# A decoder layer on one core: the first entry's order, the experts' banks and the last sums rearranged

## The chip, the core and the metric

The kernel runs on one core of a Trainium2 chip. A core has five engines with queues of their own, which meet only through semaphores: PE (TensorE: matmuls and transposes, results in PSUM), DVE (VectorE), ACT (ScalarE), POOL (GpSimd) and SP (SyncE, here only for issuing DMAs). "PEld" is PE's weight load, which overlaps its matmuls. [...] The metric is the time of one execution on the device in microseconds (us), as the median of the runs.

## The reference

A pre-norm decoder layer in float32 on 16 entries (b) of 128 tokens by 256 features:

```python
x = x + self_attention(layernorm(x))            # 16 heads of 64: q, k, v 256 -> 1024, output 1024 -> 256
x = x + cross_attention(layernorm(x), ctx, mask) # 16 heads of 16, one key mask for all entries
xf = layernorm(x).reshape(2048, 256)
logits = xf @ gate_w.T + gate_b                  # 8 experts; RMS norm, softmax at temperature 0.5
g = max(softmax(...)); norm_g = g / (g + 1e-6)   # the largest gate only
h = gelu(einsum('nd,edh->neh', xf, w1) + b1)     # all 8 experts, 512 hidden each
y = einsum('neh,ehd->ned', h, w2) + b2
x = x + (y * norm_g).sum(axis=1)                 # every expert's output counts, with one common gate
```

As every expert is used with the same factor, the experts are one two-layer network with 4096 hidden features.

## The kernel before

**Attention.** Work is cut into 16 slots, one per entry, in `slot(s)`. A slot's steps are not issued where they stand in the code. `at(name, f, ...)` puts each into one heap with a due time, slot number x SLOT (28.2 us) + `DUE[name]`, and `run_slots` then issues all steps of all slots in the order of their due times. Since PE, DVE, ACT and POOL run under `manual_schedule`, that order is the order of each engine's queue. A step that evacuates a PSUM tile (`due`) has a due time of its own.

The names that matter here: q0, q1, k0, k1, v0, v1 are the projections of queries, keys and values in halves of 512 columns (functions `queries`, `keys`, `values`; the profile's tiles mm_qk and mm_v); q0e, ke0, ve0 and so on are their evacuations (queries on DVE, keys and values on ACT). S0 and S1 are the scores of half the heads each (tile sc). For each half, max is the negated maximum on DVE (L331), ex the exponentials on ACT in two groups of four (L337), r the reciprocal of the sums on DVE (L348) and mul the normalization on POOL (L352). T1a1 to T1b2 transpose the probabilities on PE (tr_p, L367), with copies on DVE (prT); SVa and SVb multiply with the values, SO is the output projection (mm_o, weights wo). xn1, LN1 and LN1c normalize a later entry's tokens, transpose them on PE and copy them out on ACT. "early" stands for the statistics of entries 2 and 3, a chain of small DVE operations; st0 to st11 are the others' statistics.

Ahead of the slots, without due times, stand the first entry's steps in program order: normalization of entry 0, its transposes (tr_x), then keys half 0, queries half 0, normalization of entry 1, keys half 1, queries half 1, values, with entry 1's transposes between. Slot 0 then starts with both halves of the scores. The weights wq and wk are loaded in quarters of 256 columns, wq by SP's queue, wk by ACT's; rowv (biases by row, spread to all partitions) and small bias columns (bqk) by POOL's. For every engine's DMAs the queue's order is the program's.

**Experts.** Tokens go in four blocks m of 512, hidden features in 16 pairs of blocks p. Each 2x2 block product is made by seven products in place of eight (a Strassen scheme): `hidden_first` and `hidden_last` make the hidden sums in banks ha, hb, he, hf, with sums u on DVE between and factors t after the GELUs; `summed(ns, ...)` adds the products numbered ns of the second layer into eight half-banks, two in each of the four tiles y0 to y3, by `ORDER = (2, 3, 4, 8, 1, 7, 5, 6)`: products 2 and 3 share y0, 4 and 8 y1, 1 and 7 y2, 5 and 6 y3. Product 8 occurs only where the first blocks were made plainly (m = 0). The second layer's products of step p are issued in the step after it. When block m - 1 is complete, in step p = 0 of block m (a seam), `finished` makes the final sums yT straight from the half-banks, one copy on ACT and seven or eight sums on DVE; `rest`, in steps 1 and 2, transposes half of yT on PE into the bank of "he", scales with the gate, adds the residual into ot on DVE and stores it. In the experts only PE has an order written out (`manual_schedule(engines={PE})`); DVE and ACT are ordered by the framework's scheduler, which starts ready operations by priority, earlier program order first. The framework also makes every reader and writer of one bank wait for each other.

Of the kernel before, what the change touches and what calls it, by code (L numbers as in the profile page):

```python
# [65 lines left out]
    cross=13.9, st0=14.3, st1=14.8, st2=15.6, st3=16.2, st4=17.4, st5=17.9, st6=18.4, st7=18.9,  # L66
    st8=20.0, st9=20.5, st10=21.0, st11=21.5, late=31.7,
)
PRE_STEPS = ("q0", "k0", "v0", "q1", "v1", "k1")
LATE_STATS = tuple(f"st{n}" for n in range(B - 4))  # L70

# [2 lines left out]
def decoder_layer(  # L74
# [57 lines left out]
    make_identity(nc, ident)  # L132


    xs = const.tile([P, B, D], F32, tag="xs", name="xs")
    wq = keep.tile([P, KD, HD1], F32, tag="k0", name="wq")
    wk = keep.tile([P, KD, HD1], F32, tag="k1", name="wk")
# [10 lines left out]

    load_tokens(0, 1)
    nc.scalar.dma_start(out=colv, in_=cols)  # L150
    for n in range(4):
        for w, src, q in ((wq, wq1, nc.sync), (wk, wk1, nc.scalar)):
            f = slice(n * 256, (n + 1) * 256)
            q.dma_start(out=w[:, :, f], in_=src[:, :, f])
    load_tokens(1, 1)
    for n in range(2):
        f = slice(n * 512, (n + 1) * 512)
        nc.sync.dma_start(out=wv[:, :, f], in_=wv1[:, :, f])
    nc.gpsimd.dma_start(out=rowv, in_=rows.partition_broadcast(P))
    nc.gpsimd.dma_start(out=msk, in_=mask)  # L160

    bqk2 = const.tile([P, 2, C2], F32, tag="bqk2", name="bqk2")
    for n, c0 in enumerate((BQ2, BK2)):
        for m in range(C2):
            for f in range(2):
                nc.gpsimd.dma_start(
                    out=bqk2[64 * f : 64 * f + 64, n, m : m + 1],
                    in_=cols[:, c0 + 2 * m + f : c0 + 2 * m + f + 1].rearrange(
                        "(a s) o -> a s o", s=32
                    )[:, :DH2],  # L170
                )
    def context(g):
        c = work.tile([P, KD, GT], F32, tag="ctx", name=f"ctx{g}")
        nc.sync.dma_start(out=c, in_=ctxT[g])
        return c
# [58 lines left out]
    def at(name, f, *a):  # L234


        if now[0] is None:
            f(*a)
        else:
            heapq.heappush(events, (now[0] * SLOT + DUE[name], next(count), now[0], f, a))  # L240

    def due(name, f, *a):

        if now[0] is None:
            with urgent():
                f(*a)
        else:
            at(name, f, *a)

    count = itertools.count()  # L250

# [121 lines left out]
    def self_norm(b):  # L373
        entry["xn1", b] = normalize(b, *first[b])

    def self_norm_transposed(b):
        xnT1 = ap.tile([P, KD, 1, T], F32, tag="xnT1", name="xnT1")
        transpose_tokens([entry.pop(("xn1", b))], xnT1, "LN1c")
        entry["xnT1", b] = xnT1

    def project(b, w, n, tag):
# [14 lines left out]
                )  # L396
        return entry[tag, b], mm

    def queries(b, n):
        qT, mm = project(b, wq, n, "qT")  # L400
        due(
            f"q{n}e",
            nc.vector.tensor_tensor,
            qT[:, 4 * n : 4 * n + 4, :],
            mm,
            col(BQ1 + 4 * n, 4).unsqueeze(2).broadcast_to([P, 4, T]),
            ALU.add,
        )

    def keys(b, n):  # L410
        kT, mm = project(b, wk, n, "kT")

        def out():
            for i in range(4):
                c = 4 * n + i
                nc.scalar.activation(
                    kT[:, c, :], mm[:, i, :], AF.Identity,
                    bias=bk1[:, c : c + 1], scale=DH1 ** -0.5,
                )

        due(f"ke{n}", out)

    def values(b, n):
        mm = psum_mm("mm_v")
        if n == 0:
            entry["v", b] = ap.tile([P, HD1], F32, tag="v", name="v")
        f = slice(n * 512, (n + 1) * 512)
        for k in range(KD):
            nc.tensor.matmul(  # L429
                mm,  # L430
                entry["xnT1", b][:, k, 0, :],
                wv[:, k, f],
                start=(k == 0),
                stop=(k == KD - 1),
            )
        due(f"ve{n}", nc.scalar.copy, entry["v", b][:, f], mm)

    def self_scores(b, half):

# [323 lines left out]
    def slot(s):  # L763


        for half in range(2):
            at(f"S{half}", self_scores, s, half)
            at(f"SV{'ab'[half]}", self_values, s, half)
            for n in range(2):
                at(f"T1{'ab'[half]}{n + 1}", self_transposed, s, half, n)  # L770
                if s >= 2:
                    at(f"T2{'ab'[half]}{n + 1}", cross_transposed, s - 2, half, n)
        at("SO", self_output, s)
        at("cvr", cross_value_rows, s)
        at("ck", cross_keys, s)
        normalize_outputs(s, s - 2 if s >= 2 else None)
        if s >= 1:
            at("LNx", cross_norm, s - 1)
            at("CQ", cross_queries, s - 1)
            at("CS", cross_scores, s - 1)  # L780
            at("CS", cross_softmax, s - 1)
        if s >= 2:
            at("CV", cross_values, s - 2)
            at("CO", cross_output, s - 2)
        if s >= 3:
            at("LN3", expert_norm, s - 3)
        if s + 2 < B:
            at("xn1", self_norm, s + 2)
            at("ab1", add_bias, s + 2, BO1)
            at("LN1", self_norm_transposed, s + 2)  # L790
        if s + 1 < B:
            for n in range(2):
                at(f"q{n}", queries, s + 1, n)
                at(f"k{n}", keys, s + 1, n)
                at(f"v{n}", values, s + 1, n)
        else:
            for n, name in enumerate(PRE_STEPS):
                copy = nc.vector.tensor_copy if name[0] == "q" else nc.scalar.copy
                out = f"q{name[1]}e" if name[0] == "q" else f"{name[0]}e{name[1]}"
                at(name, pre_hidden, n, copy, out)  # L800
        if s == 0:
            mv2 = variances(2)
            for i in range(2):
                at(f"early{i}", statistics, mv2[:, i, :], 2 + i)
            at("early", lambda: first.update(inverse_deviations(mv2, [2, 3])))
            at("cross", for_cross)
            mv = variances(B - 4)
            for i, name in enumerate(LATE_STATS):
                at(name, statistics, mv[:, i, :], 4 + i)

            def rest():
                first.update(inverse_deviations(mv, list(range(4, B))))

            at("late", rest)
# [7 lines left out]

    first = deviations([0])
    self_norm(0)
    add_bias(0, BO1)
    self_norm_transposed(0)

    nc.vector.tensor_scalar_mul(bk1, colv[:, BK1 : BK1 + C1], DH1 ** -0.5)
    keys(0, 0)
    queries(0, 0)  # L830
    first.update(deviations([1]))
    self_norm(1)
    add_bias(1, BO1)
    keys(0, 1)
    queries(0, 1)
    values(0, 0)
    self_norm_transposed(1)
    values(0, 1)

    hidden_keys = const.tile([P, T], U8, tag="hidden_keys", name="hidden_keys")  # L840
    masked = const.tile([P, 1], F32, tag="masked", name="masked")
# [205 lines left out]
                start=cleared(i // 2, begun), stop=(p == NP - 1), skip_group_check=True,  # L1047
            )

    def finished(m, sums, plain):  # L1050
        ys = {n: sums[0][i // 2][:, i % 2] for i, n in enumerate(ORDER)}
        yT = yp.tile([P, KD, MT], F32, tag="yT", name="yT")
        u = hp.tile([P, 4, HT], F32, tag="u", name="yu")
# [1 line left out]
        def plus(out, k, y, other):  # L1055
            nc.vector.scalar_tensor_tensor(out, y, b2[:, k : k + 1], other, ALU.add, ALU.add)  # L1056

        nc.scalar.copy(u[:, 0], ys[1])
        nc.vector.tensor_add(u[:, 1], u[:, 0], ys[6])
        nc.vector.tensor_add(u[:, 2], u[:, 1], ys[7])  # L1060
        nc.vector.tensor_add(u[:, 3], u[:, 1], ys[5])
        plus(yT[:, 0, :HT], 0, ys[2], u[:, 0])
        plus(yT[:, 0, HT:], 0, ys[3], u[:, 3])
        if plain:
            plus(yT[:, 1, :HT], 1, ys[4], u[:, 2])
            nc.vector.tensor_add(u[:, 2], u[:, 2], ys[8])
            plus(yT[:, 1, HT:], 1, ys[5], u[:, 2])
        else:
            plus(yT[:, 1, HT:], 1, ys[5], u[:, 2])
            plus(yT[:, 1, :HT], 1, ys[4], u[:, 2])  # L1070

        def rest(i, bank):
            tr = ps_h.tile([P, 4, P], F32, tag=bank, name="tr_y")
            for j in range(2):
# [29 lines left out]
    def experts():  # L1104
# [1 line left out]


        nonlocal ys
        rest = None
        xr = token_factors(0)  # L1110
        combine(2)
        combine(3)
# [4 lines left out]
        for m in range(NT // MT):  # L1117
            for p in range(0 if m else PRE, NP):
# [11 lines left out]
                    lgT = gate_logits()  # L1130
                if m == 0 and p == PRE + 3:
                    gate_transposed(lgT)
                if before is None:
                    summed_plain(1, PRE - 1, ys)
                else:
                    summed((7, 5, 6, 4), *before, ys)
                    if before[0] == NP - 1:
                        rest = finished(m - 1, ys, m == 1)
                if m == 0 and p in (PRE, PRE + 1):
                    combine(p - PRE)  # L1140
                if m == 0 and p == PRE + 3:
                    gates()
                if p in (1, 2) and rest is not None:
                    rest(p - 1, "he")
                before = now
        summed((1, 5, 7, 6, 2, 3, 4), *before, ys)
        rest = finished(m, ys, False)
        for i, bank in enumerate(("hb", "hf")):
            rest(i, bank)

# [66 lines left out]
```

## Time and profile before

| | us |
|---|---|
| median of 3 runs | 876.49 (876.48 to 878.98) |
| the profiled execution's own time | 877.13 |
| its span, first to last instruction | 875.3 |
| PE busy | 856.2 |
| DVE busy | 627.5 |
| ACT busy | 425.5 |
| POOL busy | 166.8 |

In the profile's lines, L390 is line 390 of the kernel, `out<-in` names tiles, "128x512 f32" are partitions and elements, and what stands in brackets is the idle time of the engine just before and what ended it. A timeline line gives start, length of the merged group, engine, line, operation, tiles and count. The chain that ended last is followed back from the last instruction, each time to what released it; its lines give start, length and engine.

### The profile page before, as it was taken

The numbers are of one execution on the slowest core, as the hardware profiler recorded it, in microseconds if no ns is written. First come the engines' busy times: TensorE is split into PE (matmuls) and PEld (weight loads), VectorE is DVE, ScalarE is ACT, GpSimd is POOL, SyncE is SP. The second block draws the span as 40 slices with busy tenths as digits, with TensorE's granted clock in tenths as the row PEclk, the third lists the DMA queues.
The fourth block names the chain that finished last, engine by engine and source line by source line (L and its number), as shares of the span: only waits on it lengthen the run. The fifth ranks groups of instructions, "written<-read, shape, count | busy, mean of one in ns | idle before, by whom it ended". The sixth has DMA issues, their size and how long they took to land.

```text
span 875.3 us, 15944 instructions
## 1 busy us (share of the span) xinstructions
PE 856.2 (98%) x5940; PEld 713.6 (82%) x5940; DVE 627.5 (72%) x1513; ACT 425.5 (49%) x1623; POOL 166.8 (19%) x179
## 2 busy tenths in 40 slices
PE   6999999999999999999999999999999999999997
PEld 5788888888888888888865558878888888878886
DVE  3887787878878787878877497775567656575655
ACT  2356755577565765567554613333333333433332
POOL 4224423343333423343231100000000000000000
PEclk9999999999999999999999999999999999999999
DMA  8800000000000000000140100000000000000000
GB/s 220 253 1 14 1 14 2 2 13 2 13 2 2 13 2 1 14 2 1 51 177 15 49 0 1 1 25 1 0 1 1 25 0 1 1 13 13 0 1 25
DMA packets 19406, 21.29 MB, mean 24 GB/s; under 512 B 9649, under 2 KB 15809, under 8 KB 18689
## 3 DMA queue, kind: packets, MB, share of 16 engines
q1 hardware_dynamic: 17728, 18.89, 6.9%
q10 hardware_dynamic: 1232, 1.09, 0.5%
q8 instruction: 47, 0.77, 0.4%
q0 software_dynamic: 368, 0.30, 0.3%
q14 instruction: 31, 0.25, 0.1%
HBM read 18.16 MB, written 2.10 MB: 23 GB/s over the span
## 4 chain that ended last, share of the span: by engine, by line
PE 89%; DVE 7%; issue 1%; ACT 1%; DMA 1%; POOL 0%; DVEq 0%; ACTq 0%; POOLq 0%
PE y L1004 18%; PE mm_qk L390 13%; PE mm_v L429 6%; PE tr_p L367 6%; PE mm_o L489 6%; PE he L1004 5%; PE hf L1004 5%; PE ha L1004 5%; PE sc L445 4%; PE po L469 3%; PE mm_h L753 3%; PE hb L1004 2%; PE sc L579 2%; PE po L618 2%; PE mm_q L557 2%; PE y L894 2%
## 5 line engine op out<-in xcount | busy, mean ns | idle before, releaser
L352 POOL TENSOR_TENSOR cpr<-cpr,rinv 128x512 f32<-128x512 f32 x64 | 68.5, 1072 | 219.6 <-DVE rinv L348 219.3
L337 ACT ACTIVATE cpr<-sc,nmax 128x128 f32<-128x128 f32 x256 | 89.9, 411 | 11.6 <-DVE nmax L331 11.6
L337 ACT ACTIVATE pr<-sc,nmax 128x128 f32<-128x128 f32 x256 | 90.8, 420 | 1.8 <-DVE nmax L331 1.8
L352 POOL TENSOR_TENSOR pr<-pr,rinv 128x512 f32<-128x512 f32 x64 | 66.0, 1043 | 74.6 <-DVE rinv L348 74.3
L331 DVE TENSOR_REDUCE nmax<-sc 128x8 f32<-128x1024 f32 x64 | 76.4, 1216 | 4.7 <-PE sc L445 4.7
L1034 DVE TENSOR_TENSOR c<-u,hf 128x256 f32<-128x256 f32 x56 | 23.6, 421 | 72.0 <-PE hf L1004 71.9
L1033 ACT ACTIVATE h<-u,colv 128x256 f32<-128x256 f32 x56 | 28.4, 507 | 88.2 <-DVE u L1020 86.4
L390 PEld LDWEIGHTS mm_qk<-xnT,wk 128*128 128x128 f32 x512 | 62.5, 196 | 9.2 <-issue 6.4
L258 ACT COPY xnT<-tr_x 128x256 f32<-128x256 f32 x42 | 15.6, 372 | 109.5 <-PE tr_x L316 109.5
L1004 PE MATMUL hf<-xt,w 128*128 128x256 f32 x224 | 66.9, 380 | 0.4 <-DVE u L1019 0.4
L1004 PE MATMUL y<-t,w 128*128 128x256 f32 x224 | 66.7, 379 | 0.0
L1004 PE MATMUL ha<-xnT,w 128*128 128x256 f32 x224 | 66.6, 379 | 0.0
L337 ACT ACTIVATION_READ_ACCUMULATOR pr<-sc,nmax 128x1 f32 x256 | 66.3, 259 | 0.0
L390 PE MATMUL mm_qk<-xnT,wk 128*128 128x128 f32 x512 | 64.2, 280 | 1.7 <-DMA wk<-in_wk 1.7
L337 ACT ACTIVATION_READ_ACCUMULATOR cpr<-sc,nmax 128x1 f32 x256 | 64.4, 251 | 0.0
L390 PE MATMUL mm_qk<-xnT,wq 128*128 128x128 f32 x512 | 64.2, 279 | 0.0
L1017 ACT COPY u<-ha 128x256 f32<-128x256 f32 x56 | 20.9, 373 | 86.8 <-PE ha L1004 86.8
L390 PEld LDWEIGHTS mm_qk<-xnT,wq 128*128 128x128 f32 x512 | 60.1, 193 | 3.0 <-issue 2.9
L429 PE MATMUL mm_v<-wv,xnT 128*128 128x512 f32 x128 | 60.2, 592 | 0.0
L1004 PE MATMUL y<-h,w 128*128 128x256 f32 x224 | 58.7, 381 | 1.5 <-DVE yT L1056 1.1
L489 PE MATMUL mm_o<-wo,atT 128*128 128x256 f32 x256 | 57.9, 379 | 0.0
L258 DVE COPY prT<-tr_p 128x512 f32<-128x512 f32 x64 | 39.7, 682 | 18.6 <-PE tr_p L367 18.6
(167 smaller groups left out, 1864.9 us busy)
## 6 DMA issues: line engine op xcount, KB each, us to landing
w<-in_w SPq DMA_DIRECT2D x8, 1024.0 KB, 5.4
ctx<-in_ctxT SPq DMA_DIRECT2D x8, 256.0 KB, 2.7
out_x<-ot SPq DMA_DIRECT2D x8, 256.0 KB, 2.2
xs<-in_x SPq DMA_DIRECT2D x3, 512.0 KB, 5.3
wk<-in_wk ACTq DMA_DIRECT2D x4, 256.0 KB, 8.5
wq<-in_wq SPq DMA_DIRECT2D x4, 256.0 KB, 10.2
wv<-in_wv SPq DMA_DIRECT2D x2, 512.0 KB, 7.7
wo<-in_wo SPq DMA_DIRECT2D x1, 1024.0 KB, 8.3
```

Source lines behind the costliest of these rows:

```text
L258: f(*a)
L331: nc.vector.tensor_reduce(w["nmax"], sc, AX.X, ALU.max, negate=True)
L337: nc.scalar.activation(w["pr"][:, i, :], sc[:, i, :], AF.Exp, bias=w["nmax"][:, i : i + 1], scale=1.0, accum_out=sums[:, j : j + 1],)
L352: nc.gpsimd.tensor_tensor(four, four, w["rinv", n].unsqueeze(2).broadcast_to([P, 4, T]), ALU.mult)
L367: nc.tensor.transpose(tr[:, j, :], w["pr"][:, 4 * n + j, :], ident)
L390: nc.tensor.matmul(mm[:, i, :], w[:, k, c * P : (c + 1) * P], xnT1[:, k, 0, :], start=(k == 0), stop=(k == KD - 1),)
L429: nc.tensor.matmul(mm, entry["xnT1", b][:, k, 0, :], wv[:, k, f], start=(k == 0), stop=(k == KD - 1),)
L445: nc.tensor.matmul(sc[:, j, c * T : (c + 1) * T], qT[r, 4 * half + c, :], kT[r, 4 * half + c, :], start=True, stop=True,)
L469: nc.tensor.matmul(po[j * DH1 : (j + 1) * DH1, c, :], v[:, h * DH1 : (h + 1) * DH1], prT[:, 4 * j + c, :], start=True, stop=True,)
L489: nc.tensor.matmul(mm[:, :D], atT[:, c, :], wo[:, c, :], start=(c == 0), stop=(c == C1 - 1))
L1004: nc.tensor.matmul(out, left[p // q][n - 1][:, p % q], rights[n - 1], **flags)
L1033: nc.scalar.activation(h[:, 1, 1], u[:, 3], AF.Gelu, bias=col(B1 + 2 * p + 1))
```

## The change

1. Loads: wk and wq in halves of 512 columns, all by SP's queue, wk's half before wq's, entry 1's tokens after the first pair; rowv after the small bqk loads on POOL's queue.
2. A tile of zeros is set on DVE first, and PE multiplies it eleven times by itself into a bank nobody reads.
3. The first entry's steps go into the heap as well, under slot 0, with due times of their own (FIRST_DUE, negative for those before the slots). Scores of half 0 come right after keys and queries of that half and keys of the next; the softmax steps of slot 0 have new due times. The additions of the output bias to entries 0 and 1 (fab0, fab1) come after the normalizations on POOL.
4. At a seam, `emptied` copies y0, y2 and y3 out on ACT and y1 on DVE, with high priority; `summed_up_later` makes the sums from the copies, one step later. `rest` follows in steps 2 and 3, between `hidden_last` and the second layer's last products, into the bank of "hb".
5. After the last step, `summed_last` issues the products in the order 1, 6, 2, 7, 4, 5, 3 with the sums between them.

```diff
+FIRST_DUE = dict(
+    fk0=-11.4, fq0=-9.5, fk0e=-9.4, fq0e=-7.7, fk1=-7.2, norm1=-7.0, S0=-5.4, fk1e=-5.3, fq1=-4.4,
+    max0=-4.0, ex0a=-2.7, fLN=-2.65, fq1e=-2.6, fv0=-2.3, fLNc=-1.4, r0a=-1.32, ex0b=-1.3,
+    mul0a=-1.2, S1=-0.6, fv0e=0.1, r0b=0.15, mul0b=0.2, max1=0.4, fv1=0.41, ex1a=1.65, fv1e=3.0,
+    r1a=3.1, mul1a=3.2, ex1b=3.6, cvre=5.0, r1b=5.1, mul1b=5.2, fab0=5.5, fab1=6.5,
 )
...
+    zeros = work.tile([P, T], F32, tag="xnT2", name="zeros")
+    nc.vector.memset(zeros, 0.0)
+    mm = psum_mm("mm_0")
+    for n in range(11):
+        nc.tensor.matmul(mm[:, :T], zeros, zeros, start=True, stop=True)
...
-    for n in range(4):
-        for w, src, q in ((wq, wq1, nc.sync), (wk, wk1, nc.scalar)):
-            f = slice(n * 256, (n + 1) * 256)
-            q.dma_start(out=w[:, :, f], in_=src[:, :, f])
-    load_tokens(1, 1)
+    for n in range(2):
+        f = slice(n * 512, (n + 1) * 512)
+        for w, src in ((wk, wk1), (wq, wq1)):
+            nc.sync.dma_start(out=w[:, :, f], in_=src[:, :, f])
+        if n == 0:
+            load_tokens(1, 1)
...
-    nc.gpsimd.dma_start(out=rowv, in_=rows.partition_broadcast(P))
     nc.gpsimd.dma_start(out=msk, in_=mask)
...
+    nc.gpsimd.dma_start(out=rowv, in_=rows.partition_broadcast(P))
...
+    def when(name):
+        s = now[0]
+        return s * SLOT + (FIRST_DUE[name] if s == 0 and name in FIRST_DUE else DUE[name])
...
         if s == 0:
+            for n in range(2):
+                at(f"fk{n}", keys, 0, n, "fk{}e")
+                at(f"fq{n}", queries, 0, n, "fq{}e")
+                at(f"fv{n}", values, 0, n, "fv{}e")
+                at(f"fab{n}", add_bias, n, BO1)
+            def second():
+                first.update(deviations([1]))
+                self_norm(1)
+            at("norm1", second)
+            at("fLN", self_norm_transposed, 1, "fLNc")
...
     self_norm(0)
-    add_bias(0, BO1)
     self_norm_transposed(0)
...
-    keys(0, 0)
-    queries(0, 0)
-    first.update(deviations([1]))
-    self_norm(1)
-    add_bias(1, BO1)
-    keys(0, 1)
-    queries(0, 1)
-    values(0, 0)
-    self_norm_transposed(1)
-    values(0, 1)
...
+    def emptied(sums, plain):
+        y0, y1, y2, y3 = sums[0]
+        yT = yp.tile([P, KD, MT], F32, tag="yT", name="yT")
+        u = rp.tile([P, 4, HT], F32, tag="xt", name="yu")
+        y4_8 = yT[:, 1].rearrange("p (n t) -> p n t", n=2)
+        with tc.high_priority():
+            nc.scalar.activation(
+                yT[:, 0].rearrange("p (n t) -> p n t", n=2), y0, AF.Identity, bias=b2[:, 0:1]
+            )
+            nc.scalar.copy(u[:, 0:2], y2)
+            nc.scalar.copy(u[:, 2:4], y3)
+            n = 2 if plain else 1
+            nc.vector.tensor_scalar_add(y4_8[:, :n], y1[:, :n], b2[:, 1:2])
+        return yT, u, plain
+
+    def summed_up_later(yT, u, plain):
+        y1, y7, y5, y6 = (u[:, n] for n in range(4))
+        def plus(y, other):
+            nc.vector.tensor_add(y, y, other)
+        plus(y6, y1)
+        plus(y7, y6)
+        plus(yT[:, 0, :HT], y1)
+        plus(yT[:, 1, :HT], y7)
...
+        plus(y5, y6)
+        plus(yT[:, 0, HT:], y5)
+        return yT
+
+    def summed_last(p, hr, sums):
...
+        completed(1)
         nc.scalar.copy(u[:, 0], ys[1])
+        completed(6)
         nc.vector.tensor_add(u[:, 1], u[:, 0], ys[6])
+        completed(2, 7)
         nc.vector.tensor_add(u[:, 2], u[:, 1], ys[7])
+        plus(yT[:, 0, :HT], 0, ys[2], u[:, 0])
+        completed(4)
+        plus(yT[:, 1, :HT], 1, ys[4], u[:, 2])
+        completed(5)
         nc.vector.tensor_add(u[:, 3], u[:, 1], ys[5])
+        plus(yT[:, 1, HT:], 1, ys[5], u[:, 2])
+        completed(3)
         plus(yT[:, 0, HT:], 0, ys[3], u[:, 3])
...
+                if p == 1 and out is not None:
+                    rest = finished(m - 1, summed_up_later(*out))
+                if p in (2, 3) and rest is not None:
+                    rest(p - 2, "hb")
...
                     if before[0] == NP - 1:
-                        rest = finished(m - 1, ys, m == 1)
+                        out = emptied(ys, m == 1)
...
-                if p in (1, 2) and rest is not None:
-                    rest(p - 1, "he")
...
-        summed((1, 5, 7, 6, 2, 3, 4), *before, ys)
-        rest = finished(m, ys, False)
+        rest = finished(m, summed_last(*before, ys))
```

More of the change, by code (lines that the diff above doesn't have):

```diff
@@ L239, in at @@
         else:
-            heapq.heappush(events, (now[0] * SLOT + DUE[name], next(count), now[0], f, a))
+            heapq.heappush(events, (when(name), next(count), now[0], f, a))
     def due(name, f, *a):
@@ L374, in self_norm, with self_norm_transposed @@
         entry["xn1", b] = normalize(b, *first[b])
-    def self_norm_transposed(b):
+    def self_norm_transposed(b, name="LN1c"):
         xnT1 = ap.tile([P, KD, 1, T], F32, tag="xnT1", name="xnT1")
-        transpose_tokens([entry.pop(("xn1", b))], xnT1, "LN1c")
+        transpose_tokens([entry.pop(("xn1", b))], xnT1, name)
         entry["xnT1", b] = xnT1
@@ L397, in project, with queries @@
         return entry[tag, b], mm
-    def queries(b, n):
+    def queries(b, n, name="q{}e"):
         qT, mm = project(b, wq, n, "qT")
         due(
-            f"q{n}e",
+            name.format(n),
             nc.vector.tensor_tensor,
@@ L408, in queries, with keys @@
         )
-    def keys(b, n):
+    def keys(b, n, name="ke{}"):
         kT, mm = project(b, wk, n, "kT")
@@ L419, in out, with values @@
                 )
-        due(f"ke{n}", out)
-    def values(b, n):
+        due(name.format(n), out)
+    def values(b, n, name="ve{}"):
         mm = psum_mm("mm_v")
@@ L435, in values @@
             )
-        due(f"ve{n}", nc.scalar.copy, entry["v", b][:, f], mm)
+        due(name.format(n), nc.scalar.copy, entry["v", b][:, f], mm)
     def self_scores(b, half):
@@ L1048, in summed @@
             )
-    def finished(m, sums, plain):
+    def emptied(sums, plain):
[6 more added lines that the diff above has]
+                yT[:, 0].rearrange("p (n t) -> p n t", n=2), y0, AF.Identity, bias=b2[:, 0:1]
+            )
+            nc.scalar.copy(u[:, 0:2], y2)
[11 more added lines that the diff above has]
+        plus(yT[:, 1, :HT], y7)
+        if plain:
+            plus(y7, y5)
+            plus(yT[:, 1, HT:], y7)
+        else:
+            nc.vector.scalar_tensor_tensor(
+                yT[:, 1, HT:], y5, b2[:, 1:2], y7, ALU.add, ALU.add
+            )
+        plus(y5, y6)
+        plus(yT[:, 0, HT:], y5)
+        return yT
+    def summed_last(p, hr, sums):
         ys = {n: sums[0][i // 2][:, i % 2] for i, n in enumerate(ORDER)}
@@ L1056, in plus, with completed, finished @@
             nc.vector.scalar_tensor_tensor(out, y, b2[:, k : k + 1], other, ALU.add, ALU.add)
+        def completed(*ns):
+            summed(ns, p, hr, sums)
+        completed(1)
         nc.scalar.copy(u[:, 0], ys[1])
+        completed(6)
         nc.vector.tensor_add(u[:, 1], u[:, 0], ys[6])
+        completed(2, 7)
         nc.vector.tensor_add(u[:, 2], u[:, 1], ys[7])
+        plus(yT[:, 0, :HT], 0, ys[2], u[:, 0])
+        completed(4)
+        plus(yT[:, 1, :HT], 1, ys[4], u[:, 2])
+        completed(5)
         nc.vector.tensor_add(u[:, 3], u[:, 1], ys[5])
-        plus(yT[:, 0, :HT], 0, ys[2], u[:, 0])
+        plus(yT[:, 1, HT:], 1, ys[5], u[:, 2])
+        completed(3)
         plus(yT[:, 0, HT:], 0, ys[3], u[:, 3])
[L1064 to L1070, printed above, removed]
+        return yT
+    def finished(m, yT):
         def rest(i, bank):
@@ L1108, in experts @@
         nonlocal ys
-        rest = None
+        rest = out = None
         xr = token_factors(0)
```

## The prediction, made before the result was known

> **What bounds the kernel now.** I read the page first (busy shares and slices), then who waits for whom on PE, the timeline of the first 40 us, the chain that ended last through the experts, and the timeline of the last 10 us. The page:
>
> ```profile
> PE 856.2 (98%) x5940; PEld 713.6 (82%) x5940; DVE 627.5 (72%) x1513; ACT 425.5 (49%) x1623; POOL 166.8 (19%) x179
> ...
> PE   6999999999999999999999999999999999999997
> ```
>
> PE is the bound: 856.2 of 875.3 us, and only the first and last slice are thin. An edit that leaves PE's work alone can win only the 19 us in which PE stands still, and whatever of its busy time is slower than it need be. PE's waits name the first places:
>
> ```profile
> PE tr_x L316 <- DVE bk L828: 6.2, 1, 6.2
> PE mm_qk L390 <- DMA wk<-in_wk: 1.7, 1, 1.7
> PE tr_p L367 <- POOL pr L352: 1.5, 1, 1.5
> ```
>
> The timeline of the start (start, length of the group, engine, line, operation):
>
> ```profile
> 6.91 0.37 ACT L246 COPY xnT<-tr_x 128x256 f32<-128x256 f32 x1 [1.36 <-PE tr_x L316]
> ...
> 8.56 3.75 PE L390 MATMUL mm_qk<-xnT,wk 128*128 128x128 f32 x16 [1.69 <-DMA wk<-in_wk]
> ...
> 14.13 1.95 PE L390 MATMUL mm_qk<-xnT,wk 128*128 128x128 f32 x16
> ```
>
> The same sixteen matmuls take 3.75 us at first and 1.95 us later: one at a time they come every 0.213 us up to 12.53, every 0.112 us after. PE runs at half rate for 4.0 us. Then the softmax of the first entry:
>
> ```profile
> 31.73 0.17 DVE L348 RECIPROCAL rinv<-sums 128x4 f32<-128x4 f32 x1
> ...
> 32.17 2.48 DVE L258 COPY prT<-tr_p 128x512 f32<-128x512 f32 x4
> ...
> 33.21 0.66 PE L367 MATMUL tr_p<-ident,pr 128*128 128x128 f32 x4 [1.51 <-POOL pr L352]
> ```
>
> The last reciprocal of the first entry comes only at 31.73, behind the early statistics on DVE; POOL then normalizes, and PE waits. In the experts the chain that ended last shows the rhythm:
>
> ```profile
> 757.95 1.73 PE y L1004 x8
> ...
> 763.99 1.73 PE y L1004 x8
> ...
> 777.10 1.73 PE y L1004 x8
> ...
> 783.88 1.73 PE y L1004 x8
> ```
>
> A step of two hidden blocks takes 763.99 - 757.95 = 6.04 us. Across the seam two steps take 13.11 instead of 12.08; the step with four transposes of outputs takes 6.78, of which the transposes are 0.44. The end, by the timeline:
>
> ```profile
> 866.29 0.37 ACT L1058 COPY yu<-y 128x256 f32<-128x256 f32 x1 [2.11 <-PE y L1004]
> ...
> 867.87 1.65 DVE L1056 SCALAR_TENSOR_TENSOR yT<-y,b,yu 128x256 f32<-128x256 f32 x4
> ...
> 869.57 0.98 PE L1077 MATMUL tr_y<-ident,yT 128*128 128x128 f32 x7 [0.85 <-DVE yT L1056]
> 870.16 1.66 DVE L1081 SCALAR_TENSOR_TENSOR ot<-tr_y,gn,xs 128x256 f32<-128x256 f32 x4 [0.64 <-PE tr_y L1077]
> ```
>
> After the last product (867.55 to 867.93) DVE alone sets the end.
>
> The sum is made against the profiled execution: span 875.3, time 877.13, so 1.83 lie around the span. The median of the runs is 876.49, 0.64 lower; I carry the difference over to it.
>
> **Part 1, loads.** wk and wq go in halves of 512 columns, all on SP's queue, wk's first half right behind the tokens; the 264 KB of rowv go behind the small bqk loads. Before, wk's first quarter was issued at 1.19 and landed at 8.43, beside wq and rowv: rowv's packets of 4224 bytes took 360 to 540 ns each from 3 to 6 us. Now 128 KB of tokens (landed at 3.0) and 512 KB come in order. SP's queue alone moved 360 to 380 KB per us from 13 to 17 us, so the half needs about 1.5 us more; at the 160 GB/s of the stretch from 2 to 4 us it needs 3.3 and lands at 6.3. Both ends are ahead of the transposed tokens on ACT (6.91 + 0.37), so keys start at 7.33 instead of 8.56: **-1.2**. The later halves (wq at 9.1, wk 10.9, wq 13.7, wv from 15.7) stay ahead at 210 GB/s or more (2.9 MB by 15.7, from 2.0 on). On SP's queue each issue costs 0.4 to 0.9 us and waits for no engine; on ACT four issues go. POOL's queue has rowv's issue (0.74) ahead of its memsets (2.1); its first normalization is not before 17 us, so nothing waits. rowv itself is first used by add_bias, now behind the fourth normalization.
>
> **Part 2, the first entry's order.** PE's own work from the first keys to the last probability transposes is 6 projections of keys or queries at 1.78, 3 of values at 1.72, scores 2.06, cross rows 0.87, transposes 2.0 = 20.8 us at full rate, against 25.3 before (8.56 to 33.87): 4.5 lost, 1.85 of it by 18 matmuls at half rate. But with scores split and moved forward the chain through DVE and ACT is what ends last, so I follow that, from rows: keys and queries 7.33 to 10.9; queries' copy on DVE 0.69, to 11.7; norm1, the whole chain of small operations (14.94 to 17.93), 3.0, to 14.7, and the first maximum is queued behind it; maximum 1.2, to 15.9; eight exponentials (1.4 per four) with the copy of tokens between, to 19.2; the reciprocal 0.2 and second maximum 1.2, behind it in order, to 20.7; exponentials, a copy of values and exponentials, 3.4, to 24.1; last reciprocal, 24.3 (before: 31.9). Then DVE has the queries' copy 0.69, statistics 1.15, twelve small operations of 0.2, and xn 0.41: to 29.0; the four copies of transposes 2.5, to 31.5 (before 34.65). What follows on DVE (statistics, attention biases) is unchanged, so the first output product, 37.80 before, comes at 34.65. PE waits some 2 us for DVE in that stretch, where it waited 2.6 before. Its weights wo landed at 34.40 even with the old loads, so they don't hold it. From there DVE was dense (9.4 of 10 us from 30 to 40) and moves with PE. Sum of parts 1 and 2 with the full clock from the first keys on: **-3.15**.
>
> **Part 3, zeros.** One memset and eleven matmuls of zeros while PE waits for tokens (nothing until 6.21), so they cost nothing; at 0.213 each they fill 2.35 us, about 1.0 to 3.4. Whether they bring the clock is the open price: none of the 1.85, or all of it; a loss isn't excluded either, since the runs of before lie 2.5 us apart and the half rate may last longer in some. The rows need 4.0 us of work to reach the full rate; 2.35 are 0.58 of that, so I take **1.0 of 1.85**: parts 1 to 3 together are -2.3, between 0 and -3.2.
>
> [...]
>
> **Part 4, seams.** Lost today: 13.11 - 12.08 = 1.03 at two seams, 1.23 at the first (565.41 to 578.72), 3.3 in all; and 6.78 - 6.04 - 0.44 = 0.30 at each of six transposes, because "he" is needed 1.3 us after them and DVE reads it until then: 1.8. Together 5.1. The change copies the banks out: three copies of 128x512 on ACT (0.59 by the copy of values), 1.8 of the 3.7 us that ACT has free in a step; one on DVE, 0.4 to 0.7. The first bank is needed 8 matmuls, 1.73 us, after the last product, and only bank 1 is completed by that; so PE does not wait. The eight sums are then plain adds of 0.34 to 0.42, 2.7 to 3.4, in place of seven or eight that held the banks; DVE is busy 3.8 of 6.04 in a step, so they spread over two steps. They stand beside u's sums, which end 1.3 us before PE needs them (u at 861.30, he at 862.59): that cover holds single adds, and what exceeds it is PE's. I take 0.2 per seam. New is a wait: the sums' tile now shares two buffers with the tokens' factors, so factors of the next block may have to wait for the last product on the old ones; 2.16 us lie between that and the first use, and three subtractions and two adds need 1.9: 0 to 0.5 at two seams, I take 0.1. With "hb", needed 2.16 us after the transposes, the six 0.30 go. **-4.3**, between -2.5 and -5.1.
>
> **Part 5, the end.** Products of one bank hold each other's readers: the copy of product 1 started at 866.29, when 7, its neighbour in the bank, was done, though 1 ended at 865.34. In the new order 1, 6, 2, 7, 4, 5, 3 the copy starts at 865.43; product 6 waits 0.2 for its factor (DVE, 865.31); 7 and 5 wait for readers already done. DVE: u1 866.04, the first yT 866.46, u2 866.9, then one of 0.42 or 0.47 after the other until the last yT, 868.96 (before 869.52). The first two transposes' inputs are ready at 867.8, so outputs run on from there: last at 870.6 instead of 871.82. **-1.2**, between -0.5 and -1.5.
>
> **Sum**: -2.3 - 4.3 - 1.2 = -7.8: span 867.5, time 869.3 in a profiled execution, median 868.7.
>
> **Rivals.** (a) The zeros do not bring the clock, the rest holds: 1.0 later, 869.7; where the half rate lasts longer than in the profiled execution, up to 1.5 more (of the 2.5 us between the runs of before), 871.2. For it: 2.35 against 4.0 us. (b) Start and end hold, but the copies bring half the seams: DVE's orders in the experts are a scheduler's, not written out, so adds may fall ahead of u's. 876.5 - 2.3 - 1.2 - 2.0 = 871.0. (c) Slower: at a seam DVE takes the high-priority copy of bank 1 early, waits for the last product (1.3 us by the gap 571.9 to 573.2), copies (0.7) and runs all eight adds (3.4) ahead of the next u's. That is 5.4 against a cover of 1.3: 4.1 at each of three seams, 12.3 instead of 5.1, so +7.2 - 2.3 - 1.2 = +3.7, 880.2. It decides once a block of over 4.2 us stands ahead of u's (loss per seam above 2.9). Against it: in the seams before, DVE's sums stood between the others' operations, none as a block. (d) The first entry wins nothing because its chain on DVE is no shorter: 876.5 - 5.5 = 871.0; against it speaks the reciprocal's 31.73, held behind the statistics by order alone.
>
> **How the numbers follow.** Forecast 45%, (a) 25%, (b) 10%, (d) 7%, (b) and (d) together 5%, (c) 8%. A measurement tells the median from no change by about 0.3%, 2.6 us, so faster is below 873.9. The best ends (-3.2, -5.1, -1.5) give 866.7; (a) at its worst, (b) and (d) lie below 871.3, and each with the end's term at its lower bound below 872. The range is 866.6 to 872.6. Outside lie (c) and (b) with (d), 876.5 - 2.0 - 1.2 = 873.3, or 874.0 with the end's lower bound: I count those 5% as no change. Faster 0.87, same 0.05, slower 0.08.
>
> **What would show it.** Right: first keys at 7.3; the matmuls of the first keys every 0.112 us (zeros work) or 0.213 (rival a); last reciprocal of the first entry near 24.3, first output product near 34.7; two steps across a seam 12.1 to 12.4, steps with transposes 6.5; from the last product to the last output 2.7 us or less. Wrong: keys waiting for weights beyond 7.5, PE waiting on u at the seams, PE in the first slot waiting for statistics beyond 35.

## The result, and the profile after

The changed kernel takes 868.20 us (median of 5 runs, 868.07 to 868.62) against 876.54 (876.48 to 878.98): ratio 0.990, 95% interval 0.9886 to 0.9915, 8.3 us less. The forecast was 868.7. The profiled execution took 868.20, with a span of 866.1 instead of 875.3. The page after:

```profile
PE 856.7 (99%) x5962; PEld 718.1 (83%) x5962; DVE 627.8 (72%) x1517; ACT 429.1 (50%) x1629; POOL 166.5 (19%) x179
```

PE is as busy as before (856.7 against 856.2, though 22 records of zeros were added); the span shrank round it. The timeline of PE and DVE in the first 35 us:

```profile
1.06 4.85 PE L146 MATMUL mm<-zeros 128*128 128x128 f32 x22 [1.06 <-DVE zeros L143]
...
7.21 2.05 PE L410 MATMUL mm_qk<-xnT,wk 128*128 128x128 f32 x16 [0.46 <-ACT xnT L262]
...
11.44 2.02 PE L410 MATMUL mm_qk<-xnT,wk 128*128 128x128 f32 x16 [0.39 <-DMA wk<-in_wk]
...
24.30 0.18 DVE L368 RECIPROCAL rinv<-sums 128x4 f32<-128x4 f32 x1 [1.71 <-ACT pr L357]
...
29.32 2.48 DVE L278 COPY prT<-tr_p 128x512 f32<-128x512 f32 x4
...
30.65 2.28 PE L489 MATMUL po<-prT,v 128*64 128x128 f32 x32 [0.16 <-DVE prT L278]
...
34.75 3.62 PE L509 MATMUL mm_o<-wo,atT 128*128 128x256 f32 x16
```

Keys start at 7.21 and run at full rate from the first (2.05 for sixteen, 3.75 before). The first output product, on which both kernels can be laid over each other, comes at 34.75 instead of 37.80, which in the timeline of before is this line:

```profile
37.80 3.62 PE L489 MATMUL mm_o<-wo,atT 128*128 128x256 f32 x16
```

The chain through the first seam:

```profile
562.54 1.73 PE y L1025 x8
...
574.63 1.73 PE y L1025 x8
...
581.11 1.73 PE y L1025 x8
```

Two steps across the seam take 574.63 - 562.54 = 12.09 us, two plain ones 12.08; a step with transposes takes 6.48, which is 6.04 and the 0.44 of the transposes. Nothing is lost at a seam any more. The end, by the timeline:

```profile
857.44 0.70 PE L1025 MATMUL y<-t,w2c 128*128 128x256 f32 x2
...
860.29 0.87 DVE L1115 SCALAR_TENSOR_TENSOR yT<-y,b,yu 128x256 f32<-128x256 f32 x2
861.08 1.71 DVE L1146 SCALAR_TENSOR_TENSOR ot<-tr_y,gn,xs 128x256 f32<-128x256 f32 x4
```

The outputs (L1146) follow the sums without the gap of before. The last products of y start at 863.18 before, with 12.15 us to the end of the span, and at 855.25 after, with 10.81; the chains that ended last have these lines, before and after:

```profile
863.18 3.47 PE y L1004 x16
...
855.25 2.16 PE y L1025 x10
```

So the span's 9.27 us (875.33 to 866.06) are 3.05 up to the first output product, 5.06 at the three seams, 1.34 at the end, less 0.18 given back between.

### The profile page after: what moved, and what is told of

Its sections match the earlier page's. It is cut to its first block, busy times and chain, and to the rows that moved or that the text cites. A ratio compares the mean times of both kernels' runs of the same rounds, so it can differ in the third digit from the quotient of the medians.

```text
span 866.1 us, 15987 instructions
## 1 busy us (share of the span) xinstructions
PE 856.7 (99%) x5962; PEld 718.1 (83%) x5962; DVE 627.8 (72%) x1517; ACT 429.1 (50%) x1629; POOL 166.5 (19%) x179
## 4 chain that ended last, share of the span: by engine, by line
PE 90%; DVE 6%; ACT 1%; DMA 1%; issue 1%; SPq 0%; POOL 0%; DVEq 0%; POOLq 0%
PE y L1025 19%; PE mm_qk L410 12%; PE mm_o L509 6%; PE tr_p L387 6%; PE mm_v L449 6%; PE he L1025 5%; PE hf L1025 5%; PE ha L1025 5%; PE sc L465 4%; PE po L489 3%; PE mm_h L773 3%; PE hb L1025 3%; PE sc L599 2%; PE po L638 2%; PE y L915 2%; PE mm_q L577 2%
```

## The experiments

Each run is the changed kernel (one: the kernel before) with one thing altered, or two where the text says so. Three numbers read from each trace carry the comparison: the start of the first keys, the start of the first output product, and what lies between that and the end of the span. The last column is the time, median (range). The kernel before took 875.71 to 879.53 in the later runs beside these, with medians of 878.4 to 878.9 and not 876.54, so times are compared with the changed kernel's; against those medians the change is worth some 10 us (after_again: ratio 0.988).

| kernel | first keys | first output product | from there to the end | time |
|---|---|---|---|---|
| before | 8.56 | 37.80 | 837.53 | 876.54 (876.48 to 878.98) |
| changed | 7.21 | 34.75 | 831.31 | 868.20 (868.07 to 868.62) |
| no_zeros | 7.33 | 35.94 | 831.34 | 869.30 (869.04 to 870.42) |
| zeros_5 | 7.62 | 37.02 | 831.34 | 870.06 (869.39 to 870.72) |
| old_loads | 8.72 | 37.38 | 831.57 | 870.88 (870.40 to 871.59) |
| old_loads_more_zeros | 8.98 | 38.96 | 831.25 | 870.91 (870.36 to 872.33) |
| old_order | 7.34 | 35.44 | 831.17 | 869.00 (868.39 to 869.50) |
| old_seams | 7.16 | 34.70 | 836.35 | 872.98 (872.58 to 873.23) |
| rest_late | 7.04 | 34.35 | 833.08 | 869.68 (869.59 to 869.83) |
| old_tail | 7.05 | 34.27 | 832.39 | 868.63 (868.45 to 868.76) |
| early_stats | 7.15 | 33.28 | 831.28 | 866.61 (866.50 to 867.06) |
| zeros_before | 8.25 | 40.07 | 837.44 | 877.29 (875.43 to 879.34) |
| after_again | 7.17 | 34.72 | 831.30 | 868.14 (867.62 to 868.49) |
| early_stats_again | 7.03 | 33.16 | 831.32 | 867.01 (866.67 to 867.34) |

The column before the time separates the edits cleanly: it is 831.2 to 831.6 wherever the experts are as changed, whatever happened in the first 40 us.

**no_zeros**

```diff
-    for n in range(11):
-        nc.tensor.matmul(mm[:, :T], zeros, zeros, start=True, stop=True)
```

> The changed kernel without the memset and the matmuls of zeros. Theory (the zeros bring PE to its full rate before the first keys): the first keys come every 0.213 us again and some 18 of them cost 0.10 us each more, so the time is 868.2 + 1.85 = 870.1, up to 871.6 if the half rate lasts longer than the 4.0 us seen before the change. Rival (DVE's chain of norm1 and maxima hides it, or the rate would have risen anyway): 868.2, within 0.4.

The first keys by PE's timeline:

```profile
7.33 3.61 PE L405 MATMUL mm_qk<-xnT,wk 128*128 128x128 f32 x16 [0.47 <-ACT xnT L257]
10.78 1.95 PE L405 MATMUL mm_qk<-xnT,wq 128*128 128x128 f32 x16
```

The half rate is back (3.61 for sixteen, 2.05 in the changed kernel), and the first output product is 1.19 us later, the time 1.1. The rival falls. The theory's 1.85 was too much: from the first keys to the queries it is 3.45 us (7.33 to 10.78) instead of 1.89 (7.21 to 9.10), 1.56 more, the queries ran at full rate (1.95), and 0.39 of wk's wait at 11.44 in the changed kernel was no longer felt.

**zeros_5**

```diff
-    for n in range(11):
+    for n in range(5):
```

> Five matmuls of zeros instead of eleven: ten records of 0.213 us, 2.1 us from 1.06 on. Theory (a stretch of about 4 us of work is needed): the full rate does not come before the first keys at 7.2, time as without zeros, 870.1. Rival (any early work counts; the blind estimate's proportion, half of the work for half of the gain): 868.2 to 869.2, with the first keys every 0.112 us for at least a part.

```profile
1.06 2.51 PE L146 MATMUL mm<-zeros 128*128 128x128 f32 x10 [1.06 <-DVE zeros L143]
6.50 0.66 PE L336 MATMUL tr_x<-ident,xn 128*128 128x128 f32 x2 [2.94 <-DVE bk L859]
7.62 3.79 PE L410 MATMUL mm_qk<-xnT,wk 128*128 128x128 f32 x16 [0.46 <-ACT xnT L262]
11.20 2.61 PE L410 MATMUL mm_qk<-xnT,wq 128*128 128x128 f32 x16
```

2.5 us of zeros helped no more than none: 3.79 for the first sixteen, and 2.61 for the queries behind them (1.95 in no_zeros). This is about the amount of work that the prediction had reckoned with, and it brings nothing in this trace; eleven calls are 22 records and 4.85 us.

**old_loads**

```diff
-    for n in range(2):
-        f = slice(n * 512, (n + 1) * 512)
-        for w, src in ((wk, wk1), (wq, wq1)):
-            nc.sync.dma_start(out=w[:, :, f], in_=src[:, :, f])
-        if n == 0:
-            load_tokens(1, 1)
+    for n in range(4):
+        for w, src, q in ((wq, wq1, nc.sync), (wk, wk1, nc.scalar)):
+            f = slice(n * 256, (n + 1) * 256)
+            q.dma_start(out=w[:, :, f], in_=src[:, :, f])
+    load_tokens(1, 1)
...   # rowv ahead of msk again
```

> The changed kernel with the loads of before: wq and wk in quarters on SP's and ACT's queue, entry 1's tokens behind them, rowv ahead of mask and bqk. Theory (keys started with the landing of wk): first keys at 8.4 to 8.6 instead of 7.21, time 868.2 + 1.3 = 869.5; if the later quarters hold keys half 1 and queries half 1 too, up to 870.5. Rival (DVE's chain hides the later start): 868.2, within 0.4.

Keys start 1.51 us later, but the first output product comes 2.63 later and the time is 2.7 higher, above the theory's range. What was added is the clock. The clock that was granted to PE, by stretches (stretch, length, busy time and count of PE, PEld, DVE, ACT and POOL, then PEclk, DMA share and GB/s):

```profile
6.60:9.90 3.30, 1.35 (x12) 1.22 (x11) 0.00 (x0) 0.37 (x1) 0.61 (x1) 1.00 1.17 306
9.95:13.30 3.35, 3.35 (x18) 3.35 (x17) 0.00 (x0) 1.14 (x4) 2.65 (x4) 0.50 1.14 308
13.40:20.00 6.60, 6.60 (x60) 5.88 (x60) 5.05 (x15) 2.17 (x10) 0.00 (x0) 1.00 0.94 263
```

The zeros had brought the full rate, and it was lost again at 9.92 for 3.41 us, after PE, but for two transposes, had stood from the zeros' end to 8.72; in old_loads_more_zeros, where zeros fill 1.73 us of that, no key was slow. DVE's chain starts with the copy of the queries:

```profile
14.19 0.69 DVE L276 TENSOR_TENSOR qT<-mm_qk,colv 128x512 f32<-128x512 f32 x1 [8.02 <-PE mm_qk L408]
14.80 0.42 DVE L306 BATCH_NORM_STATS2 st<-xs 128x6 f32<-128x256 f32 x1
```

It comes 3.10 us later than in the changed kernel (11.09): 1.51 by the keys' start and 1.6 by the matmuls at half rate (2.45 us for the keys and 2.82 for the queries, 8.72 to 11.17 to 13.99, against 1.89 in the changed kernel and 1.78 in no_zeros); 0.5 is made up further on. Entry 1's tokens, landed at 14.72, held nothing here. The new loads differ in four things (halves, one queue, their order, rowv's place), which were not tried apart.

**old_loads_more_zeros**

```diff
+    mm = psum_mm("mm_1")
+    for n in range(7):
+        nc.tensor.matmul(mm[:, :T], zeros, zeros, start=True, stop=True)
     nc.vector.tensor_scalar_mul(bk1, colv[:, BK1 : BK1 + C1], DH1 ** -0.5)
```

> The changed kernel with the loads of before, and seven more matmuls of zeros behind the first transposes, from 6.9 to 8.5, so that PE works on until the keys. Theory (with the old loads alone the full rate was lost at 9.92 and came back at 13.33, sixteen matmuls at half rate, 1.7 us, because PE stood from 5.9 to 8.7): no key or query at 0.213 us, the first output product near 37.38 - 1.7 = 35.7, the time near 869.2. Rival (the late second halves of the weights hold PE, not the rate): as with the old loads alone, 870.9, within 0.5.

No key or query was slow (2.02 us for the first sixteen keys, 1.95 for the next), as the theory said, and still the time is the rival's, though not for its reason. The queries' copy comes 0.72 us earlier than in old_loads, but what follows it on DVE doesn't; its timeline:

```profile
13.47 0.69 DVE L276 TENSOR_TENSOR qT<-mm_qk,colv 128x512 f32<-128x512 f32 x1 [7.29 <-PE mm_qk L408]
15.03 0.43 DVE L306 BATCH_NORM_STATS2 st<-xs 128x6 f32<-128x256 f32 x1 [0.87 <-DMA xs<-in_x]
```

With the old loads entry 1's tokens land at 15.00, and the normalization, ahead of the first maximum in DVE's order, waits for them. So what the new loads bring is not the weights alone. The normalization starts 3.33 us later than in the changed kernel (15.03 against 11.70): 2.38 of it is the later copy of the queries (13.47 against 11.09), the weights' part, and 0.95 the tokens', which in the changed kernel go between the halves and landed at 9.06. This run's first output product, 38.96, is later than old_loads' mainly because the full rate was lost once more:

```profile
28.00:33.50 5.50, 3.58 (x22) 2.34 (x20) 4.98 (x20) 1.49 (x6) 2.55 (x4) 1.00 1.05 393
33.60:36.90 3.30, 3.30 (x32) 3.20 (x32) 3.15 (x14) 0.23 (x1) 0.00 (x0) 0.50 1.03 405
```

PE had waited 1.8 us for DVE's copies of the transposes, and what came next, from 33.60 to 36.90, ran at half rate (0.50). This execution was the slowest of the four (872.33, granted clock 0.998); the others took 870.36 to 871.23 at 1.000, a mean over the span that leaves no room for this loss.

**zeros_before** (the kernel before, with the zeros only)

```diff
+    zeros = work.tile([P, T], F32, tag="xnT2", name="zeros")
+    nc.vector.memset(zeros, 0.0)
+    mm = psum_mm("mm_0")
+    for n in range(11):
+        nc.tensor.matmul(mm[:, :T], zeros, zeros, start=True, stop=True)
```

> The kernel before with only the memset and the eleven matmuls of zeros added; keys still start with wk's landing near 8.6. [...] Rival (the rate stays once reached): all at 0.112 us, the first output product at 37.80 - 1.85 = 35.95, the time 1.8 us below before.

```profile
4.00:7.00 3.00, 1.55 (x12) 1.14 (x11) 1.83 (x10) 1.66 (x2) 2.42 (x5) 1.00 0.92 211
7.40:14.10 6.70, 5.85 (x27) 5.88 (x28) 0.00 (x0) 1.14 (x4) 3.95 (x6) 0.50 1.15 307
14.20:34.60 20.40, 18.54 (x138) 14.47 (x137) 13.37 (x42) 10.08 (x45) 5.72 (x6) 1.00 0.96 254
34.70:38.00 3.30, 3.30 (x32) 3.20 (x32) 3.15 (x14) 0.37 (x1) 0.00 (x0) 0.50 1.03 406
```

The full rate was lost before the first keys (0.50 from 7.40 to 14.10, with the keys from 8.25 on), and again after PE's wait of 1.51 us for POOL's last normalization (0.50 from 34.70 to 38.00); the first output product comes at 40.07, later than without zeros. This execution was the slowest of ten (879.34; the fastest took 875.43). The median, 877.29, is inside the range of the kernel before (ratio 0.999, interval 0.9975 to 1.0005). So no gain of the zeros can be told here, though by the times alone the rival's 1.8 us (ratio 0.998) isn't excluded; what speaks against its reason is the trace, where the rate, 1.00 from 4.00 to 7.00, does not stay once reached.

**old_order**

```diff
-            for n in range(2):
-                at(f"fk{n}", keys, 0, n, "fk{}e")
...
+    keys(0, 0)
+    queries(0, 0)
+    first.update(deviations([1]))
...   # the program order of before, FIRST_DUE empty
```

> The changed kernel with the first entry's steps in program order ahead of the slots and no FIRST_DUE, but the new loads and the zeros. Theory (the order shortens the chain through DVE and ACT): the last reciprocal of the first entry comes 2 us or more later than 24.30, the first output product 1.5 to 2.5 us later than 34.75, time 869.7 to 870.7. Rival (the earlier start, 1.35, and the clock, 1.85, are all of the 3.05 us at the first output product, and the order is worth nothing): first output product at 34.6, time 868.2 within 0.4.

Between the two: the first output product comes 0.69 us later (0.13 of it because keys start later, wk's half having landed at 7.20), the time is 0.8 higher. The last normalization on POOL starts 5 us later than in the changed kernel (24.56 there), as the theory said, and PE waits for it again, but the copies of transposes are only 0.50 later:

```profile
29.62 1.18 POOL L367 TENSOR_TENSOR pr<-pr,rinv 128x512 f32<-128x512 f32 x1 [2.16 <-DVE rinv L363]
29.82 2.48 DVE L273 COPY prT<-tr_p 128x512 f32<-128x512 f32 x4
30.85 0.42 PEld L382 LDWEIGHTS tr_p<-ident,pr 128*128 128x128 f32 x4 [1.76 <-POOL pr L367]
```

In the old order the early statistics stand ahead of the last reciprocal, in the new one behind it, and either way ahead of the copies. The new order moved 5 us of wait from one place to another and kept 0.7 at most. Two of the four executions took 868.4 to 868.5 us at a granted clock of 0.999 and 1.000, two 869.5 at 0.998; whether PE's wait for POOL cost the rate in these two, no trace here shows.

**early_stats**, made to test that reading and to be better than both

```diff
     r1a=3.1, mul1a=3.2, ex1b=3.6, cvre=5.0, r1b=5.1, mul1b=5.2, fab0=5.5, fab1=6.5,
+    early0=1.5, early1=1.55, early=3.15,
```

> An attempt at a better kernel: the changed one with early0 and early1 due at 1.5 and 1.55 and early at 3.15 in slot 0, so that the statistics of entries 2 and 3 run in DVE's idle time between the second maximum (ends 20.83) and the last reciprocal (24.30). Theory (that chain, 24.97 to 28.99, holds back the four copies of transposes, and these the products with the values): copies start near 27.8 instead of 29.32, the first output product 1.3 us earlier, or 0.9 where wo's landing at 33.5 holds it; time 867.0 to 867.4. Rival (DVE is dense up to 45 us, so what is moved comes back later): 868.2, within 0.3.

```profile
27.83 2.48 DVE L279 COPY prT<-tr_p 128x512 f32<-128x512 f32 x4 [1.06 <-PE tr_p L388]
```

The time is 866.61, a little below the theory's range. DVE now waits 1.06 us for PE there, no longer the other way round. The copies start 1.49 us earlier, the first output product 1.47, and nothing comes back later (831.28). DVE's idle time while it waits for ACT's exponentials had been free.

**after_again and early_stats_again**, side by side

> The changed kernel once more, beside the next one on the same chip. Every theory: 868.2, within 0.4.

> The version with the statistics of entries 2 and 3 in DVE's idle time, once more, to be compared with the changed kernel on the same chip. Theory (first output product 1.47 us earlier, and nothing given back later): 1.4 to 1.7 us below the changed kernel, 866.6. Rival (the difference in the call before came from the first tokens' landing): within 0.4 of the changed kernel.

867.01 against 868.14, with ranges that don't touch (866.67 to 867.34, 867.62 to 868.49); the spans differ by 1.54. Against the kernel before the ratios are 0.9872 (0.9855 to 0.9888) and 0.9883 (0.9868 to 0.9898). The median's 1.1 is a little under the 1.4 expected; the version is the fastest one here.

**old_seams**

```diff
-                if p == 1 and out is not None:
-                    rest = finished(m - 1, summed_up_later(*out))
-                if p in (2, 3) and rest is not None:
-                    rest(p - 2, "hb")
...
-                        out = emptied(ys, m == 1)
+                        rest = finished(m - 1, summed_up_now(ys, m == 1))   # the sums of before
...
+                if p in (1, 2) and rest is not None:
+                    rest(p - 1, "he")
```

> The changed kernel with the seams of before: sums straight from the banks in step 0, transposes at the end of steps 1 and 2 into the bank of he. Start and end stay changed. Theory (the seams' 5.06 us come from the banks and the transposes' place alone): two steps across a seam 13.1 to 13.3 again, steps with transposes 6.78, time 868.2 + 5.1 = 873.3. Rival (part of it came from the start having shifted the loads of the experts' weights): below 872.5.

Two steps across the first seam take 13.31 us again (562.48 to 575.79), the two steps with transposes 6.78 each. From the first output product to the end it is 836.35 instead of 831.31: 5.04, all of the seams' 5.06. The start doesn't bear on it.

**rest_late**

```diff
-                if p in (2, 3) and rest is not None:
-                    rest(p - 2, "hb")
...
+                if p in (2, 3) and rest is not None:
+                    rest(p - 2, "he")    # at the end of the step
```

> The changed kernel with the copies out of the banks kept, but the output transposes again at the end of the step, behind the second layer's products, into the bank of he (steps 2 and 3). Theory (the place decides: he is needed 1.3 us after the transposes and DVE reads it longer): each of six steps 6.78 instead of 6.48, time 868.2 + 1.8 = 870.0. Rival (the 0.30 came from the eight sums of before crowding DVE, not from the place): 868.2 to 868.6.

The chain at the first seam:

```profile
562.13 1.73 PE y L1025 x8
...
574.21 1.73 PE y L1025 x8
580.26 1.73 PE y L1025 x8
...
587.04 1.73 PE y L1025 x8
```

The seam stays free (12.08 for two steps), the step with transposes takes 6.78, and from the first output product to the end it is 1.77 longer. So of the 5.04, 1.77 belong to the transposes' place with its bank (both went back together), and the other 3.27 to the copies with the later sums.

**old_tail**

```diff
-        rest = finished(m, summed_last(*before, ys))
+        summed((1, 5, 7, 6, 2, 3, 4), *before, ys)
+        rest = finished(m, summed_up_now(ys, False))
```

> The changed kernel with the end of before: last products in the order 1, 5, 7, 6, 2, 3, 4, the sums after them. Theory (the order lets the sums run between the products): from the first of the last products to the end of the span 12.1 instead of 10.85, time 868.2 + 1.3 = 869.5. Rival (most of the end is the stores, 2.2 us from issue to landing and what follows): 868.2 to 868.6.

By the time alone, 868.63, it would be the rival. But this execution's first output product was 0.48 us early, as its loads were: the first tokens landed 0.17 us earlier than in the changed kernel's trace, wk's second half, for which PE waited there, 0.47 (10.84 against 11.31). From the first output product to the end it is 1.08 longer. The end is worth 1.1.

## Why the prediction was right, point by point

**Loads.** Keys came 1.35 us earlier, 1.2 were forecast. wk's half landed at 6.93, later than the 6.3 of the bound, 0.28 ahead of its use; wk's second half held PE for 0.39, which I had excluded. The run old_loads shows that the loads are worth 2.63 at the first output product, 1.6 of it through the rate that was lost there (0.50 from 9.95 to 13.30), which this term didn't have; entry 1's tokens, which it didn't count either, held the chain 0.9 where the rate was kept (old_loads_more_zeros). The packets of rowv that part 1 puts at 360 to 540 ns each took that in the mean of each microsecond; single ones took 164 to 1185.

**The first entry's chain.** The steps added up from rows gave 24.3 for the last reciprocal, 31.5 for the end of the copies and 34.65 for the first output product; they came at 24.30, 31.80 and 34.75. Following the order of DVE and ACT was right where counting PE's 4.5 lost us would have been wrong; PE waited 0.8 for DVE's copies there, less than the 2 of the prediction. My own sum left 0.1 for the order itself (1.2 and 1.85 of 3.15), and against rival (d) I argued with the reciprocal's 31.73 as if that were a gain. By old_order it is not: 5 us at the reciprocal are 0.7 at most at the first output product. Rival (d) as a whole fell all the same, as without the order the start still wins 2.36 (35.44 against 37.80).

**Zeros.** This is the term that was mis-sized. Eleven calls were taken as eleven records of 0.213; each left two in the trace (22), which the sixteen records for eight calls of keys in the trace of before would have told. They fill 4.85 us, not 2.35, and the full rate was there at 5.56, before the first keys; rival (a) fell. By zeros_5 the reckoned 2.35 would have brought nothing: with 2.51 us of zeros the first sixteen keys took 3.79. The price was off too: without the zeros the first output product is 1.19 later, not 1.85, as the slow keys cost 1.56, and part of that went into a wait for wk that was there anyway. So the 1.0 in the sum came near the 1.19 by two errors against each other, which is luck.

**Seams.** 5.04 against 4.3 within 2.5 to 5.1. The 0.2 per seam for crowding on DVE and the 0.1 for the shared buffer did not occur. The timeline of DVE after the first seam shows why rival (c) fell:

```profile
571.75 0.41 DVE L1039 TENSOR_TENSOR u<-u,hb 128x256 f32<-128x256 f32 x1
...
572.42 0.41 DVE L1040 TENSOR_TENSOR u<-u,hf 128x256 f32<-128x256 f32 x1
...
572.75 0.42 DVE L1091 TENSOR_TENSOR yu<-yu 128x256 f32<-128x256 f32 x1
...
573.09 0.41 DVE L1041 TENSOR_TENSOR u<-u,he 128x256 f32<-128x256 f32 x1
...
573.42 0.42 DVE L1091 TENSOR_TENSOR yu<-yu 128x256 f32<-128x256 f32 x1
```

The sums (L1091) went singly between u's (L1039 to L1041); u was complete at 573.50, PE needed he at 574.03. The cover of 1.3 shrank to 0.5 and held.

**The end.** 1.08 by experiment, 1.34 between the traces, 1.2 forecast. Product 6 waited 0.43 for its factor where I had 0.2. The last sum ended at 861.16, 1.2 behind the start of the last matmul of the products (859.92), where the prediction had 1.4 (868.96 and 867.55), and the outputs followed it without a gap, as worked out.

**The sum** was -7.8. In the span it came to -9.27: 0.75 more from the start (by no_zeros 0.19 of it is the zeros; loads and order together brought 1.86 without them, where the sum had 1.3), 0.76 from the seams, 0.14 from the end, less the 0.18 given back between. The profiled time fell by 8.93, as 0.34 more lies around the span now, and the median by 8.34, since the kernel before was profiled 0.59 above its median. For the profiled execution the forecast was 869.3, 1.1 above the 868.20 that came; that the median was met within 0.5 is partly luck, as the 0.64 carried over from before did not apply: the changed kernel was profiled at its median. Rival (b) fell with the seams.

## What to carry to other kernels

Where several engines' queues are in order, a wait that is moved off one engine can stand next behind another (in old_order 5 us at the reciprocal were 0.7 at most at the first output product); follow the chain through the engine that ends last, and look there for idle time, as early_stats did. Idle PE time cost twice where the clock fell back: in old_loads (0.50 from 9.95 to 13.30) keys that came 1.51 us later put the first output product back by 2.63. So the worth of early work, an unbroken PE and loads that keep it unbroken depends on each other: taken away singly, zeros, loads and order cost 1.19, 2.63 and 0.69, together more than the 3.05 that the start won. Copying a full accumulator out at once and adding later cost nothing here (12.09 us for two steps across a seam, 12.08 for two plain ones), as the copies and sums fitted between the next step's operations, with 0.5 us of cover left; count that cover in us.

## What the runs showed of the hardware

PE's matmuls of 128x128 by 128x128 came every 0.213 us or every 0.112, and the clock that the traces record as granted is 0.50 or 1.00. Where it changed, or did not:

| kernel | rate, by the trace | what PE had done before |
|---|---|---|
| before | sixteen keys from 8.56 in 3.75 us, from 14.13 in 1.95; 1.00 from 12.58 to 872.74 | waited 1.69 us up to 8.56, then worked on; waited 1.51 us up to 33.21 without a loss |
| changed | 1.00 from 5.56 to 865.72 | 4.85 us of zeros from 1.06 on |
| no_zeros | sixteen keys from 7.33 in 3.61 us, sixteen queries from 10.78 in 1.95 | nothing up to 6.20, then two transposes |
| zeros_5 | sixteen keys from 7.62 in 3.79 us, sixteen queries from 11.20 in 2.61 | 2.51 us of zeros, then a wait of 2.94 and two transposes |
| old_loads | 1.00 from 6.60 to 9.90, 0.50 from 9.95 to 13.30, 1.00 from 13.40 to 20.00 | waited 1.95 us up to 8.72 |
| old_loads_more_zeros | 1.00 from 28.00 to 33.50, 0.50 from 33.60 to 36.90, 1.00 from 37.00 to 42.00 | waited 1.8 us for DVE's copies |
| zeros_before | 1.00 from 4.00 to 7.00, 0.50 from 7.40 to 14.10 | waited 1.04 us up to 6.18 and 1.67 up to 8.25 |
| zeros_before | 1.00 from 14.20 to 34.60, 0.50 from 34.70 to 38.00, 1.00 from 38.10 to 44.00 | waited 1.51 us up to 33.81 |

The length of a wait alone does not tell whether the rate falls: with 1.51 us of waiting for POOL it fell in zeros_before and did not in the kernel before. What decides it, and how much work raises the rate, was not shown; no run was made to test it.

The kernel before spread over 3.8 us in the later runs, the changed one over 1.0 in all. The spread of the kernel before goes with the clock: of its 27 later executions, the 18 with a granted clock (mean over the span) of 0.996 took 878.05 to 879.53 us, the 9 with 0.998 took 875.71 to 877.44. By estimate, one more stretch at half rate, as long as the 3.41 us of old_loads, costs 3.41 x 0.5 = 1.7 us, or 0.002 of the span. Where in the kernel it lay is not shown, as its one trace has no such loss between 12.58 and 872.74; PE's wait of 1.51 us up to 33.21, after which zeros_before lost the rate, is a likely place.
